# A mixer's double layer norm: two square roots and a product, or one combined scale

## The chip, the cores and the metric

The kernel runs on one core of a Trainium2 chip. Its time is device microseconds of one execution, as a median over runs. The engines named below are PE (TensorE: matmuls; PEld its weight loads), DVE (VectorE), ACT (ScalarE), POOL (GpSimd) and SP (SyncE, which here issues DMAs). Each engine works through its own queue of instructions in order and waits on semaphores for the others.

## The reference

The program is two transformer-like layers over x of 4 x 1024 x 256 in float32. What matters here is the first step of layer 0, a recurrent mixer with gates. Its input is normalized twice: once by the block and once by the mixer.

```python
def _layernorm(x, axis=-1, eps=1e-05):
    m = jnp.mean(x, axis=axis, keepdims=True)
    v = jnp.var(x, axis=axis, keepdims=True)
    return (x - m) / jnp.sqrt(v + eps)
...
    # in _L0_attn_ref, EPS = 1e-05
    mu = jnp.mean(x, axis=-1, keepdims=True)
    var = jnp.mean(jnp.square(x - mu), axis=-1, keepdims=True)
    xn = (x - mu) * jax.lax.rsqrt(var + EPS) * ln_w + ln_b
    log_i, log_f, z, o = ...                # four gates, each from xn by a 256 x 64 matrix
    # a scan over the 1024 steps: m = max(m + lf, li); c = exp(..) * c + exp(..) * z; h = o * tanh(c)
    return jnp.einsum('bsn,dn->bsd', h_seq, Wp) + bp
...
x = x + _L0_attn_ref(_layernorm(x, axis=-1), ...)      # the mixer
x = x + _L0_ffn_ref(_layernorm(x, axis=-1), ...)       # 8 experts, the best 2 of each token
x = x + _L1_attn_ref(_layernorm(x, axis=-1), ...)      # attention, 16 heads
x = x + _L1_ffn_ref(_layernorm(x, axis=-1), ...)       # 32 experts, the best 4, and a shared one
```

After the first norm the mean is 0 and the variance is var / (var + eps), so that both norms together are one scale of (x - mean): with r1 = 1 / sqrt(var + eps) and r2 = 1 / sqrt(var r1^2 + eps), it is r1 r2 = 1 / sqrt(var (1 + eps) + eps^2).

## The kernel before

x stays in SBUF, one tile of 128 partitions per batch element, with two further columns of each row for its mean and its variance or scale. Layer 0 is worked in four *units*: a pair of batch elements (0 and 1, or 2 and 3) times a half of the 1024 steps, so eight tiles of 128 tokens each. `l1_unit(u)` is the mixer of a unit, `l2_route(u)` its choice of experts. The calls stand in this order: `l1_unit(0)`, `l1_unit(1)`, `l2_route(0)`, `l2_route(1)`, the lists of the tiles of the experts' queues that are full by then (A: 25 tiles), then the same for units 2 and 3 and the lists of the other tiles (B and C), and then the experts, `l2_experts`, over 68 tiles.

A mixer unit goes: `stats` (BN statistics on DVE, L260 and L261, into the columns of x); the scale, in the lines that the change touches (L304 to L312; `rstd0` has the square root on ACT in L269 and the reciprocal on DVE in L270); `transposed`, which makes xn = (x - mean) * scale on DVE (L279), transposes it on PE (L287) and copies it out on ACT with ln_w and ln_b (L316); the addition of the output's bias to x (L323); the four gates' matmuls (L334); on DVE and ACT the clipping (L340, L341), tanh and sigmoid (L343), two scans (L356, L363) and exponentials (L359, L361, L367); and the output's matmuls (L376), added to x (L383). The route of a unit goes through `stats`, `rstd0` and `transposed` as well, then router matmuls (L396), the best two of each row (L407, L410, L412), positions in the queues by matmuls (L426, L427), and DMAs on POOL that scatter the rows of x to DRAM (L245). After the last route `pn_all` (L461), the lengths of all queues, comes from PE, and DVE makes the lists B and C from it (L470 to L568).

An expert tile is loaded from DRAM by a DMA on SP (L578), normalized on DVE (L586), transposed (L591), copied (L593), and goes through the hidden layer (L608, `ph1` and `ph2`), SiLU on ACT (L613), a product on DVE (`hid`, L614), a transposition (L620, L622) and the output (L628, L632). `ph1` and `ph2` have one PSUM bank each, so that a tile's hidden layer waits for the product of the tile before. Until tile 12 the outputs share banks with the transposed inputs; from then on they have two banks that the mixer held before (`T_LATE = 12`).

The program is recorded in this order, and a scheduler then lays the instructions out for each engine: it may put the beginning of one part between the steps of another. So expert tiles of list A stand among the instructions of units 2 and 3, on PE, DVE and ACT. The order inside the experts is kept on PE. Before attention there is a branch for tiles past the 68th (L775). Attention and layer 1's experts, after it, have an order that is written out by hand; no line of them is changed.

ACT has its functions in sets; the program has a table load where the next function is not in the set that is loaded. Square root, tanh and sigmoid, exp, and SiLU alternate in this part.

Of the kernel before, what the change touches and what calls it, by code (L numbers as in the profile page):

```python
# [14 lines left out]
F32 = mybir.dt.float32  # L15
BF16 = mybir.dt.bfloat16
I32 = mybir.dt.int32
AF = mybir.ActivationFunctionType
# [5 lines left out]
P = 128  # L24
# [4 lines left out]
EPS = 1e-5  # L29
# [27 lines left out]
def block_kernel(  # L57
# [23 lines left out]
    nc = tc.nc  # L81
    const = ctx.enter_context(tc.tile_pool(name="const", bufs=1))
# [10 lines left out]
    for pr in range(B // 2):  # L93
# [6 lines left out]
    make_identity(nc, ident)  # L100
    eps_t = const.tile([P, 1], F32, name="eps_t")
    nc.gpsimd.memset(eps_t, EPS)


    lower = const.tile([P, P], F32, name="lower0")
# [2 lines left out]
        out=lower, in_=lower, compare_op=ALU.is_gt, fill=0.0, base=0,  # L108
# [68 lines left out]
    with ExitStack() as ph:  # L177
# [3 lines left out]
        sm = ph.enter_context(tc.tile_pool(name="l2_small", bufs=2))  # L181
# [8 lines left out]
        HT0 = NT // 2  # L190
# [64 lines left out]
        def stats(u, name):  # L255

            pr, hf = units0[u]
            for b, i in tiles_of(u):
                st = sm.tile([P, 6], F32, name=f"st_{name}_{b}_{i}", tag="st", bufs=4)
                nc.vector.bn_stats(st, x[b][:, i, :D])  # L260
                nc.vector.bn_aggr(x[b][:, i, D : D + 2], st)  # L261
            half = slice(hf * HT0, (hf + 1) * HT0)
            return [x[2 * pr + par][:, half, D + 1] for par in range(2)]

        def rstd0(var, out, name):

            for par in range(2):
                r = sm.tile([P, HT0], F32, name=f"r_{name}_{par}", tag="r", bufs=4)
                nc.scalar.activation(r, var[par], AF.Sqrt, bias=eps_t)  # L269
                nc.vector.reciprocal(out[par], r)  # L270

        def transposed(u, name, evacuate):

            tiles = tiles_of(u)
            for par in range(2):
                xns = []
                for b, i in tiles[par * HT0 : (par + 1) * HT0]:
                    xn = sm.tile([P, D + 2], F32, name=f"xn_{name}_{b}_{i}", tag="xn", bufs=4)[:, :D]
                    nc.vector.tensor_scalar(  # L279
                        xn, x[b][:, i, :D], x[b][:, i, D : D + 1], x[b][:, i, D + 1 : D + 2],  # L280
                        ALU.subtract, ALU.mult,
                    )
                    xns.append(xn)
                for c in range(NC_):
                    pt = ps_t.tile([P, HS], F32, name=f"pt_{name}_{par}_{c}", tag="t")
                    for q in range(HT0):
                        nc.tensor.transpose(  # L287
                            pt[:, q * P : (q + 1) * P], xns[q][:, c * P : (c + 1) * P], ident
                        )
                    evacuate(c, par, pt)  # L290
# [7 lines left out]
        def l1_unit(u):  # L298
            pr, hf = units0[u]
            nm = f"l1_{u}"  # L300
            var = stats(u, nm)


            r1 = [sm.tile([P, HT0], F32, name=f"r1_{u}_{par}", tag=f"r1_{par}") for par in range(2)]  # L304
            rstd0(var, r1, nm)
            v2 = [sm.tile([P, HT0], F32, name=f"v2_{u}_{par}", tag=f"v2_{par}") for par in range(2)]
            for par in range(2):
                nc.vector.tensor_mul(v2[par], r1[par], r1[par])
                nc.vector.tensor_mul(v2[par], v2[par], var[par])
            rstd0(v2, v2, nm + "b")  # L310
            for par in range(2):
                nc.vector.tensor_mul(var[par], v2[par], r1[par])  # L312
            xT = xtp.tile([P, 2, NC_, HS], F32, name=f"l1_xT{u}", tag="xT")
            transposed(
                u, nm,
                lambda c, par, pt: nc.scalar.activation(  # L316
                    xT[:, par, c, :], pt, AF.Identity,
                    bias=lnwb_t[:, c, 1:2], scale=lnwb_t[:, c, 0:1],
                ),
            )  # L320
            for par in range(2):
                xs = x[2 * pr + par][:, hf * HT0 : (hf + 1) * HT0, :D]
                nc.vector.tensor_tensor(  # L323
                    xs, xs, bp_t.unsqueeze(1).to_broadcast([P, HT0, D]), ALU.add
                )

            gates = [
                big.tile([P, HS], F32, name=f"l1_{n}{u}", tag=f"g_{n}") for n in ("i", "f", "z", "o")
            ]
            for g in (1, 0, 2, 3):  # L330
                pg = ps_g.tile([P, HS], F32, name=f"pg_{u}_{g}", tag="g")
                for c in range(NC_):
                    for par in range(2):
                        nc.tensor.matmul(  # L334
                            pg[par * N0 : (par + 1) * N0, :], wgate_t[:, c, g, :], xT[:, par, c, :],
                            start=(c == 0), stop=(c == NC_ - 1),
                        )
                bias = bgate_t[:, g : g + 1]
                if g < 2:
                    nc.vector.tensor_scalar(gates[g], pg, bias, -20.0, ALU.add, ALU.max)  # L340
                    nc.vector.tensor_scalar_min(gates[g], gates[g], 20.0)  # L341
                else:
                    nc.scalar.activation(  # L343
                        gates[g], pg, AF.Tanh if g == 2 else AF.Sigmoid, bias=bias
                    )
            li, lf, z, o = gates
            m = big.tile([P, HS + 1], F32, name=f"l1_m{u}", tag="m")
            cst = li
            last = sm.tile([P, 2], F32, name=f"l1_last{u}", tag="last")
            if hf == 0:  # L350
                nc.vector.memset(m[:, 0:1], 0.0)
                m0 = c0 = 0.0
            else:
                m0, c0 = carry[pr][:, 0:1], carry[pr][:, 1:2]
                nc.vector.tensor_copy(m[:, 0:1], m0)
            nc.vector.tensor_tensor_scan(m[:, 1:], lf, li, m0, ALU.add, ALU.max)  # L356
            nc.vector.tensor_add(lf, lf, m[:, :HS])
            nc.vector.tensor_sub(lf, lf, m[:, 1:])
            nc.scalar.activation(lf, lf, AF.Exp)  # L359
            nc.vector.tensor_sub(li, li, m[:, 1:])  # L360
            nc.scalar.activation(li, li, AF.Exp)  # L361
            nc.vector.tensor_mul(z, z, li)
            nc.vector.tensor_tensor_scan(cst, lf, z, c0, ALU.mult, ALU.add)  # L363
            nc.vector.tensor_copy(last[:, 0:1], m[:, HS : HS + 1])
            nc.vector.tensor_copy(last[:, 1:2], cst[:, HS - 1 : HS])
            carry[pr] = last
            nc.scalar.activation(cst, cst, AF.Tanh)  # L367
            nc.vector.tensor_mul(o, o, cst)
            for q in range(0, HT0, 2):
                pos_ = [  # L370
                    ps_g.tile([P, 2, D], F32, name=f"po_{u}_{q}_{par}", tag="g") for par in range(2)
                ]
                for k in range(2):
                    for par in range(2):
                        rows = slice(par * N0, (par + 1) * N0)
                        nc.tensor.matmul(  # L376
                            pos_[par][:, k, :], o[rows, (q + k) * P : (q + k + 1) * P],
                            wp_t[rows, :], start=True, stop=True,
                        )
                for par in range(2):  # L380
                    i = hf * HT0 + q
                    xs = x[2 * pr + par][:, i : i + 2, :D]
                    nc.vector.tensor_add(xs, xs, pos_[par])  # L383

        def l2_route(u):
            tiles = tiles_of(u)
            nm = f"l2_{u}"
            var = stats(u, nm)
            rstd0(var, var, nm)
            xT = xtp.tile([P, 2, NC_, HS], F32, name=f"l2_xT{u}", tag="xT")  # L390
            transposed(u, nm, lambda c, par, pt: nc.scalar.copy(xT[:, par, c, :], pt))
# [309 lines left out]


        l1_unit(0)
        l1_unit(1)
        l2_route(0)
        l2_route(1)
# [17 lines left out]


        l1_unit(2)
        l1_unit(3)
        l2_route(2)
# [539 lines left out]
    with ExitStack() as ph:  # L1268
        wat = ph.enter_context(tc.tile_pool(name="w_att", bufs=1))
        sm = ph.enter_context(tc.tile_pool(name="l3_small", bufs=3))  # L1270
# [14 lines left out]
            out=mask[:, 3 * P :], in_=mask[:, 3 * P :], compare_op=ALU.is_ge, fill=-MASKED, base=0,  # L1285
# [16 lines left out]
        for p in range(NP - 1):  # L1302
            for k, src in enumerate((w_q, w_k, w_v)):
                nc.sync.dma_start(
                    out=w_pairs[:, p, k], in_=src[:, :, (p + 1) * P : (p + 2) * P]
# [624 lines left out]
```

## Time and profile before

| | us |
|---|---|
| median of 5 runs | 2044.32 |
| lowest and highest | 2043.84, 2051.47 |
| the profiled execution | 2041.24 |
| its span, first to last instruction | 2039.5 |
| PE, DVE, ACT, POOL busy in the span | 1841.4, 1253.0, 959.2, 269.4 |
| mean granted clock of PE | 0.953 |
| first and last square root of the mixer and the routes (L269) | 8.0, 175.7 |
| `pn_all` on PE | 195.0 |
| first matmul of attention | 594.28 |

A span counts from the first to the last instruction of the program. In a timeline each row has the start, the time until the end of the group, the engine, the line of the kernel, the operation, output and input with shapes, the count, and in brackets the idle time of the engine before it with what ended that. A float32 matmul can be two records. PEclk and "granted clock" are shares of PE's full clock. Rows of one engine overlap a little: the next instruction starts before the last one's result is written.

### The profile page before, as it was taken

Reading aid. Unit: us, or ns where it says so; the run is one execution under the profiler, and the core shown is the slowest. Engines: PE = TensorE matmul, PEld = TensorE weight load, DVE = VectorE, ACT = ScalarE, POOL = GpSimd, SP = SyncE. Lnnn points to the kernel's source line nnn. Section 1 sums busy time; section 2 is a strip of 40 time slices with the busy share of each in tenths; the row PEclk is TensorE's granted clock in tenths of the full one; section 3 lists DMA queues with packets and bytes.
Section 4 is the critical chain, followed back from the end, with each engine's and each line's share of the span. In section 5 each row is a group of like instructions: output and inputs, shape, how many; then the busy total and the mean of one; then the engine's idle time right before and its main releaser. Section 6 shows DMA issues by size and latency. Waiting matters only on the chain.

```text
span 2039.5 us, 45184 instructions
## 1 busy us (share of the span) xinstructions
PE 1841.4 (90%) x17612; PEld 1205.4 (59%) x17612; DVE 1253.0 (61%) x4101; ACT 959.2 (47%) x2486; POOL 269.4 (13%) x307
## 2 busy tenths in 40 slices
PE   5668899999999999999998999998999999998963
PEld 2435466665656766666665666665666665665642
DVE  6687222244227777755677675577777477777566
ACT  3354222222236665763555654456565355655210
POOL 0334400022003200000003030000302003031022
PEclk8578999999999999999999999999999999999987
DMA  9122211122135433100000000000000000002135
GB/s 350 40 65 80 90 47 47 42 80 77 54 94 162 146 116 107 64 1 2 1 2 23 2 2 2 1 2 2 2 2 2 2 2 2 2 2 70 42 127 184
DMA packets 87151, 109.23 MB, mean 54 GB/s; under 512 B 13838, under 2 KB 76650, under 8 KB 85776
## 3 DMA queue, kind: packets, MB, share of 16 engines
q1 hardware_dynamic: 66528, 73.41, 10.9%
q0 software_dynamic: 15168, 27.05, 4.4%
q10 hardware_dynamic: 5232, 5.78, 0.9%
q8 instruction: 143, 2.34, 0.5%
q14 instruction: 80, 0.66, 0.1%
HBM read 51.75 MB, written 64.77 MB: 57 GB/s over the span
## 4 chain that ended last, share of the span: by engine, by line
PE 52%; DVE 12%; ACT 3%; DMA 2%; issue 1%; SPq 0%; POOL 0%; DVEq 0%; ACTq 0%; POOLq 0%
PE ps L1452 10%; PE pa L1538 9%; PE pt L1502 7%; PE pq L903 6%; PE pz L903 5%; PE pk L903 5%; PE pv L903 5%; DVE ps L1468 3%; ACT pe L1481 3%; DMA xs_d<-x,row_l 1%; PE s_l L903 1%; DVE pT L1523 1%; DVE nm L1466 1%; PE sy L903 1%; PE pb L1409 0%
## 5 line engine op out<-in xcount | busy, mean ns | idle before, releaser
L1481 ACT ACTIVATE pe<-ps,nm 128x512 f32<-128x512 f32 (+3 forms) x768 | 439.0, 578 | 287.5 <-DVE nm L1468 282.5
L1538 PE MATMUL pa<-pT,v 128*64 128x128 f32 (+1 forms) x4096 | 325.2, 291 | 0.0
L1538 PEld LDWEIGHTS pa<-pT,v 128*64 128x64 f32 x4096 | 243.4, 138 | 102.5 <-issue 84.4
L1452 PE MATMUL ps<-k,q 64*128 64x512 f32 (+3 forms) x1536 | 296.3, 502 | 0.0
L1502 PEld LDWEIGHTS pt<-ident,pe 64*128 64x128 f32 x4608 | 206.5, 141 | 115.0 <-issue 53.9
L1502 PE MATMUL pt<-ident,pe 64*128 64x64 f32 x4608 | 240.9, 230 | 28.9 <-ACT pe L1481 28.5
L608 PE MATMUL ph<-w_t,xgT 128*128 x544 | 257.7, 615 | 7.0 <-DVE hid L614 5.8
L1523 ACT COPY pT<-pt 128x512 f32<-128x512 f32 (+2 forms) x384 | 179.3, 520 | 163.9 <-PE pt L1502 162.2
L1466 DVE TENSOR_REDUCE nm<-ps 128x1 f32<-128x512 f32 x256 | 175.8, 687 | 122.7 <-PE ps L1452 121.6
L859 POOL DMA_INDIRECT xs_d<-x,row_l x104 | 103.0, 990 | 1035.5 <-DVE second L1011 984.9
L1523 DVE COPY pT<-pt 128x256 f32<-128x256 f32 (+3 forms) x384 | 178.1, 505 | 0.0
L1452 PEld LDWEIGHTS ps<-k,q 64*128 64x128 f32 x1536 | 134.2, 190 | 66.5 <-issue 54.2
L1468 DVE CUSTOM_DVE_ANT_0 ps<-ps,mask_a,nm 128x128 f32<-128x128 f32 (+3 forms) x256 | 143.2, 559 | 40.5 <-DVE nm L1466 8.5
L608 PEld LDWEIGHTS ph<-w_t,xgT 128*128 128x128 f32 x544 | 100.7, 196 | 110.1 <-issue 102.4
L1481 ACT ACTIVATION_READ_ACCUMULATOR pe<-ps,nm 128x1 f32 x768 | 152.2, 198 | 0.0
L903 PE MATMUL pq<-l_xT,w_pairs 128*64 128x512 f32 x448 | 112.5, 624 | 30.9 <-ACT pe L1481 30.9
L1468 DVE CUSTOM_DVE_ANT_0 ps<-ps,mask_a 128x128 f32<-128x128 f32 (+3 forms) x256 | 119.7, 517 | 24.2 <-PE ps L1452 22.4
L903 PE MATMUL pz<-wo_t,y 128*64 128x256 f32 x1024 | 115.0, 379 | 0.0
L903 PE MATMUL pv<-w_pairs,l_xT 128*64 128x128 f32 x1792 | 108.9, 274 | 2.9 <-ACT pe L1481 2.9
L628 PE MATMUL py<-w_t,hidT 128*128 x464 | 109.6, 379 | 0.0
L903 PE MATMUL pk<-l_xT,w_pairs 128*64 128x512 f32 x448 | 107.2, 599 | 0.5 <-ACT pe L1481 0.5
L680 POOL DMA_INDIRECT yg<-yq_d,back x64 | 60.6, 947 | 334.0 <-issue 231.1
(412 smaller groups left out, 2228.3 us busy)
## 6 DMA issues: line engine op xcount, KB each, us to landing
yt_d<-zeros SPq DMA_DIRECT2D x32, 512.0 KB, 3.2
xg<-xe_d SPq DMA_DIRECT2D x68, 129.0 KB, 2.1
yq_d<-ys SPq DMA_DIRECT2D x68, 128.0 KB, 2.0
xs_d<-zeros SPq DMA_DIRECT2D x65, 131.5 KB, 2.2
w_t<-w_dram SPq DMA_DIRECT2D x8, 1024.0 KB, 13.2
w_pairs<-e_w_dram POOLq DMA_DIRECT2D x12, 384.0 KB, 3.7
x<-x_in_dram SPq DMA_DIRECT2D x8, 512.0 KB, 8.5
w_t<-w_dram SPq DMA_DIRECT2D x8, 512.0 KB, 13.6
```

Source lines behind the costliest of these rows:

```text
L608: nc.tensor.matmul(pt, xgT[:, c, :], w[:, c, k * H0 : (k + 1) * H0], start=(c == 0), stop=(c == NC_ - 1),)
L628: nc.tensor.matmul(py, hidT[:, c, :], w[:, c, :], start=(c == 0), stop=(c == H0 // P - 1))
L680: gather = nc.gpsimd.indirect_dma_start(out=yg, out_offset=None, in_=yq_d[: rows * P, :], in_offset=bass.IndirectOffsetOnAxis(ap=back_i[:, ...
L859: i = nc.gpsimd.indirect_dma_start(out=self.out, out_offset=bass.IndirectOffsetOnAxis(ap=idx, axis=0), in_=src, in_offset=None, bounds_che ...
L903: nc.tensor.matmul(out[r], lhsT[:, r], rhs, start=start, stop=stop)
L1452: nc.tensor.matmul(t[:, :n], qs[b, p][rows, i * P : (i + 1) * P], ks[b, p][rows, kc * 512 : kc * 512 + n], start=True, stop=True,)
L1466: nc.vector.tensor_reduce(m[:, 0:1], t, AX.X, ALU.min)
L1468: nc.vector.tensor_tensor_reduce(out=t[:, :n], in0=t[:, :n], in1=mask[:, 512 - n :], scale=1.0, scalar=-LOWEST if kc == 0 else m[:, 0:1], ...
L1481: inst = nc.scalar.activation(pe[:, :n], sps.pop((u, k, par))[:, :n], AF.Exp, bias=ms[u, i, par][:, 1:2], scale=-1.0, accum_out=ls[b, p][: ...
L1502: nc.tensor.transpose(pts[u][r][:, j, par, :], pes[u, k, par][rows, j * P : (j + 1) * P], ident[rows, rows],)
L1523: copy(to, pts[u][r][:, :n])
L1538: nc.tensor.matmul(pas[0][rows, cols], vs[b, p][:, j, rows], pTs[u][:, j, par, a * P :], start=(j == 0), stop=(j == nb - 1),)
```

## The change

The two square roots, two reciprocals and three products per batch element of a unit become one square root, with a scale of 1 + EPS and a bias of EPS^2, and one reciprocal, straight into x's column. A constant tile is added for the bias.

```diff
     eps_t = const.tile([P, 1], F32, name="eps_t")
     nc.gpsimd.memset(eps_t, EPS)
+    eps2_t = const.tile([P, 1], F32, name="eps2_t")
+    nc.gpsimd.memset(eps2_t, EPS * EPS)
...
-        def rstd0(var, out, name):
+        def rstd0(var, out, name, scale=1.0, bias=eps_t):
 
             for par in range(2):
                 r = sm.tile([P, HT0], F32, name=f"r_{name}_{par}", tag="r", bufs=4)
-                nc.scalar.activation(r, var[par], AF.Sqrt, bias=eps_t)
+                nc.scalar.activation(r, var[par], AF.Sqrt, bias=bias, scale=scale)
                 nc.vector.reciprocal(out[par], r)
...
             var = stats(u, nm)
 
 
-            r1 = [sm.tile([P, HT0], F32, name=f"r1_{u}_{par}", tag=f"r1_{par}") for par in range(2)]
-            rstd0(var, r1, nm)
-            v2 = [sm.tile([P, HT0], F32, name=f"v2_{u}_{par}", tag=f"v2_{par}") for par in range(2)]
-            for par in range(2):
-                nc.vector.tensor_mul(v2[par], r1[par], r1[par])
-                nc.vector.tensor_mul(v2[par], v2[par], var[par])
-            rstd0(v2, v2, nm + "b")
-            for par in range(2):
-                nc.vector.tensor_mul(var[par], v2[par], r1[par])
+            rstd0(var, var, nm, 1.0 + EPS, eps2_t)
```

The scheduler lays the changed program out anew, so the order of instructions differs on PE, DVE and ACT in the whole of this part, not only at the edited lines; a few issues of expert rows on SP change places too. Line numbers after the edited lines are lower by 6.

## The prediction

> **What bounds the kernel now.** I read the page first, then a table of windows over the first 260 us, then the timelines of PE, DVE and ACT in that stretch, and last the order of the changed program's instructions, engine by engine. The page says that PE carries the kernel (90% busy, 52% of the chain), but its slices show that the first 250 us are another regime.
>
> ```profile
> PE   5668899999999999999998999998999999998963
> DVE  6687222244227777755677675577777477777566
> PEclk8578999999999999999999999999999999999987
> ```
>
> The edit lies in slices 1 to 5, where PE is not full and its clock is below full speed. The windows (us; busy time, count of records; granted clock; DMA) show it closer:
>
> ```profile
> core 0: us, PE busy (x) PEld busy (x) DVE busy (x) ACT busy (x) POOL busy (x), PEclk, DMA share, GB/s
> 60.00:80.00 20.00, 13.66 (x57) 10.79 (x55) 9.71 (x60) 3.54 (x6) 0.00 (x0) 0.50 0.00 0
> ...
> 100.00:120.00 20.00, 12.08 (x42) 6.34 (x43) 16.73 (x86) 3.69 (x7) 15.06 (x15) 0.61 0.28 99
> 120.00:140.00 20.00, 12.60 (x46) 6.11 (x44) 16.07 (x58) 15.26 (x19) 3.71 (x3) 0.74 0.24 73
> 140.00:160.00 20.00, 17.84 (x85) 8.16 (x84) 19.03 (x52) 15.47 (x19) 0.00 (x0) 1.00 0.06 14
> 160.00:180.00 20.00, 19.37 (x78) 13.21 (x78) 13.79 (x88) 7.75 (x13) 3.13 (x5) 0.74 0.25 57
> ```
>
> Units 0 and 1 with their routing run up to 101 us without any expert tile. From 129 us expert tiles (L591, L608, L620, L628) stand on PE between the steps of units 2 and 3, and PE is fuller and faster. The timelines give the places that decide:
>
> ```profile
> 100.60 0.57 PE L461 MATMUL pn_half<-run,ones 128*128 128x8 f32 x2
> ...
> 194.97 0.34 PE L461 MATMUL pn_all<-run,ones 128*128 128x8 f32 x2
> ...
> 207.39 3.75 PE L608 MATMUL ph<-w_t,xgT 128*128 x4 [5.83 <-DVE hid L614]
> ...
> 221.10 3.69 PE L608 MATMUL ph<-w_t,xgT 128*128 x8
> ...
> 227.94 3.69 PE L608 MATMUL ph<-w_t,xgT 128*128 x8
> ```
>
> ```profile
> 12.30 0.22 DVE L270 RECIPROCAL r<-r_l 128x4 f32<-128x4 f32 x2
> ...
> 14.19 1.05 DVE L279 TENSOR_SCALAR xn_l<-x 128x256 f32<-128x256 f32 x3
> ...
> 107.95 0.38 DVE L279 TENSOR_SCALAR xn_l<-x 128x256 f32<-128x256 f32 x1
> ...
> 206.66 0.67 DVE L614 TENSOR_TENSOR hid<-hid,ph 128x512 f32<-128x512 f32 x1
> ```
>
> After `pn_all` (195.0) DVE makes the lists of the remaining tiles in 11.5 us without a pause, and the product `hid` of expert tile 4 stands behind them, at 206.66. PE waits for it 5.83 us. From there on nothing of the mixer is left, and PE goes through tile after tile at a fixed pace: 227.94 - 221.10 = 6.84 us.
>
> **What is removed, as engine time.** Per unit two square roots on ACT (292 ns each) and eight small DVE instructions (two reciprocals, six products, about 155 ns each, 75 ns from start to start). Over four units: 8 x 0.29 = 2.3 us of ACT, 32 x 0.075 = 2.4 us of DVE. In the changed order ACT also has three table loads fewer: 3 x 1.28 = 3.8 us. The added memset on POOL is like the one of `eps_t` (0.10 us, at 1.07), in the idle time before the first x lands at 4.9: nothing, and 0.1 us without that cover. The scale is an immediate of a square root that is there anyway. A table load shows 1283 ns, and the ACTIVATE behind it starts 1.29 us after the load does.
>
> [...]
>
> **What of it is on the path.** Four places.
> - Unit 0: the first xn starts 14.19 - 12.30 = 1.9 us after the first reciprocal. In the new order two reciprocals (0.15), one BN aggregate (0.09) and two BN statistics (0.65) stand between: 0.9 us. Gain 1.0 us. Units 1 and 3 normalize beside the gates of units 0 and 2: nothing on the path.
> - Unit 2: tile 0's xn now stands ahead of the lists of the first half. The second xn takes the place behind them where the old order has unit 2's last product (107.28), and a product and a reciprocal ahead of it (104.11, 104.18; 0.15 us) are gone: 107.1 instead of 108.53. Gain 1.4.
> - Unit 2's gates: ACT waits 4.64 us for unit 3's statistics before its square root at 121.08, and the tanh gate's table load and the gate (122.69) are queued behind. In the new order that square root stands behind both gates. PE has the tanh gate's sums about 1.8 us (eight records of 0.227 us) before its end of gates at 122.8, so at 121.0. Gain 1.6.
> - DVE: unit 2's z product (129.70) is queued behind two expert rows that wait for their DMA (2.22 us idle, until 128.69). In the new order the five waiting expert rows stand behind the output gate and before the add of the output (L383): 5 x 0.32 = 1.6 us go there. A gain of some 2 and a loss of 1.6: I take 0, with 2 either way.
> Sum: 4.0 us that the end of unit 3's routing comes earlier.
>
> **What is moved.** This is the larger part and not in the diff. The order on PE is laid out by the scheduler, and the experts fall behind: before `pn_all` the old order has hidden-layer matmuls (L608) up to three of four of tile 4 and the outputs of tiles 0 and 1; the new one has L608 of tiles 0 to 2 alone, and no output. The product `hid` behind the lists on DVE is that of tile 4 in the old order and that of tile 2 in the new one. So when the 5.83 us wait ends, PE stands exactly two tiles further back. The pace of 6.84 holds until tile 12, whose outputs have banks of PSUM of their own (the pace is then 5.82: 575.81 to 581.63), so both are tiles of that pace: 2 x 6.84 = +13.7 us. PE has no free time later to hide it: from 240 to 540 us it is busy 295.85 of 300.
>
> How much earlier does the wait end? Besides the 4.0, it lacks two tiles' work on PE ahead of it. The bounds: all of it was on the path, 13.7 more; or none. The nearest row is the first pair of units, which has the same steps and no tile among them: from its first xn to `pn_half` 100.60 - 14.19 = 86.4 us; the second pair with its tiles, 194.97 - 107.95 = 87.0. The tiles cost that path 0.6 us: they filled holes, and the clock that they kept up paid for the rest. I take about 4 us in all. Net +13.7 - 4 = +9.7 us.
>
> **The clock.** In 60:80 PE is busy 13.66 of 20 us and gets 0.50; in 140:160 it is busy 17.84 and gets 1.00. Fewer tiles in 120:180 mean more time at half clock there, as in the first pair; the 86.4 us hold that already, at its worst. A further price, if the hole after `pn_all` grows or its matmuls run at half clock: the four records at 207.39 took 3.75 us, 1.8 more than the four at 199.58 (1.98); three such stretches are +5.
>
> [...]
>
> **Rivals.**
> - *The second pair is bound by PE.* For it: PE is busy 37.2 of 40 us in 140:180. Then two tiles fewer ahead of the wait bring it 13.7 us earlier, the same 13.7 come back later, and the 4.0 of the shorter chain remain: 2044.3 - 4.0 = 2040.3, not slower. Against it: 87.0 against 86.4. It decides if the wait ends over 13.7 us earlier; to show as faster it must be 19.8.
> - *Half of the moved work was on the path*: wait ends 9 to 10 us earlier, net +4, 2048.
> - *Colder*: the chain gains only unit 0's 1.0 us, and some stretches at half clock are added: +12.7 to +18, 2057 to 2062.
> - *A later stage swallows the shift*: attention's first matmuls (594.28) wait 0.83 us for the branch behind the experts and nothing else; little speaks for it.
>
> **Numbers.** The profiled execution took 2041.24 us (span 2039.5 and 1.7 around it), 3.1 below the median of five, 2044.32. With +9.7 it would be 2050.9; on the median, 2054.0, my prediction. What a measurement can tell from no change is about 0.3%, 6.1 us. Forecast, +6 to +14: 0.56. Colder: 0.18. Half, PE-bound up to 6.1 us gain, or swallowed: 0.19. Faster by more, if the chain was worth more than 4.0 and PE bound it: 0.07. Slower 0.74, same 0.19, faster 0.07. Range: up to colder's 2062, down to 2044, so that half is in and only the cases with no loss, and little above, are out.
>
> **What would show it.** Right: in the profile after, the wait of PE for `hid` (L608 in the new lines) lies some 4 us earlier than 207.39, it is tile 2's product on DVE that ends it, and two more steps at the pace of 6.84 follow than before; the experts end near 604 instead of 594; ACT has 29 table loads instead of 32 in that part. Wrong: the wait ends 10 or more us earlier, or PE shows windows with clock 1.00 in 60:120, or the experts end at 594 and the difference lies in attention.

## The result, and the profile after

The changed kernel took 2051.77 us (median of 34 runs, 2047.64 to 2057.97), the kernel before 2044.76 us in 60 runs beside it (2037.29 to 2052.64). The ratio of the runs is 1.0034 with a 95% interval from 1.0026 to 1.0042, or +7.0 us (+5.3 to +8.6): slower by 0.3%. Here and below, the us beside a ratio are that ratio taken of the median of before; the bare difference of two medians can differ from it by up to 3 us. The forecast was 2054.0, range 2044 to 2062, likeliest sign slower.

The profiled execution took 2051.93 us with a span of 2050.3, 10.8 more than the span before. The profiled execution before lay 3.5 us below its median, so the pair of traces shows more than the runs do. The page of the changed kernel, its slices:

```profile
span 2050.3 us, 45138 instructions
...
PE   5567999999999999999999999998999999998963
...
DVE  6687222234317777654677775577777477777666
...
PEclk9567999999999999999999999999999999999986
```

PE has 5 and 7 in slices 2 and 4 where it had 6 and 8, and 9 in slice 5 where it had 8; the clock has 6 and 7 in slices 3 and 4 where it had 7 and 8; DVE's first eight digits are the same. From slice 6 on PE is as full as before. The table of windows (busy time and records of each engine, granted clock, DMA) for the same stretches:

```profile
core 0: us, PE busy (x) PEld busy (x) DVE busy (x) ACT busy (x) POOL busy (x), PEclk, DMA share, GB/s
60.00:80.00 20.00, 13.31 (x55) 10.66 (x54) 9.75 (x62) 3.48 (x6) 0.00 (x0) 0.50 0.00 0
100.00:120.00 20.00, 13.16 (x48) 6.48 (x49) 16.38 (x79) 4.32 (x6) 15.29 (x16) 0.62 0.29 103
120.00:140.00 20.00, 12.20 (x45) 6.99 (x43) 18.55 (x57) 12.93 (x16) 3.60 (x3) 0.64 0.21 63
140.00:160.00 20.00, 15.89 (x71) 9.68 (x67) 12.83 (x37) 10.92 (x15) 0.00 (x0) 0.76 0.00 1
160.00:180.00 20.00, 17.71 (x57) 9.31 (x57) 15.69 (x95) 8.26 (x11) 7.27 (x9) 0.76 0.33 83
```

60:80 and 100:120 are nearly as before. From 120 on PE does less, and 140:160, which had a clock of 1.00, has 0.76. Added up from the trace's clock records, 115 to 211 us holds 41.2 us at half clock, against 31.1 before. PE's timeline:

```profile
100.01 0.54 PE L455 MATMUL pn_half<-run,ones 128*128 128x8 f32 x2
...
190.85 0.36 PE L455 MATMUL pn_all<-run,ones 128*128 128x8 f32 x2
...
203.34 3.78 PE L602 MATMUL ph<-w_t,xgT 128*128 x4 [6.97 <-DVE hid L608]
...
217.47 3.69 PE L602 MATMUL ph<-w_t,xgT 128*128 x8
...
224.30 3.69 PE L602 MATMUL ph<-w_t,xgT 128*128 x8
...
604.29 3.65 PE L897 MATMUL pq<-l_xT,w_pair 128*64 128x512 f32 x16 [0.82 <-ACTq L769]
```

`pn_all` comes 4.1 us earlier than 194.97 and the wait for `hid` ends 4.05 earlier than 207.39; the pace is still 6.83; attention starts at 604.29 instead of 594.28, 10.0 later. In DVE's timeline the first xn (L281) and the product behind the lists (L608), which is now tile 2's:

```profile
12.47 0.23 DVE L272 RECIPROCAL x<-r_l 128x4 f32<-128x4 f32 x2
...
13.32 1.04 DVE L281 TENSOR_SCALAR xn_l<-x 128x256 f32<-128x256 f32 x3
...
106.91 0.41 DVE L281 TENSOR_SCALAR xn_l<-x 128x256 f32<-128x256 f32 x1
...
202.61 0.68 DVE L608 TENSOR_TENSOR hid<-hid,ph 128x512 f32<-128x512 f32 x1
```

ACT's timeline at the gates of unit 2: the square root of unit 3 (L271) now stands behind both gates, but ahead of the exponentials.

```profile
119.97 0.69 ACT L337 ACTIVATE l_z<-pg,bgate_t 128x512 f32<-128x512 f32 x1 [3.93 <-PE pg L328]
...
123.97 0.30 ACT L271 ACTIVATE r_l<-x,eps_t 128x4 f32<-128x4 f32 x1
124.29 1.28 ACT L353 ACT_TABLE_LOAD   x1
125.58 0.63 ACT L353 ACTIVATE l_f<-l_f 128x512 f32<-128x512 f32 x1
```

The tanh gate is 2.7 us earlier than its 122.69 before, the exponential only 1.1 earlier than its 126.69.

### The profile page after: what moved, and what is told of

It is laid out like the page before. It is cut to its first block, busy times and chain, and to the rows that moved or that the text cites. A ratio compares the mean times of both kernels' runs of the same rounds, so it can differ in the third digit from the quotient of the medians.

```text
span 2050.3 us, 45138 instructions
## 1 busy us (share of the span) xinstructions
PE 1847.3 (90%) x17612; PEld 1208.2 (59%) x17612; DVE 1250.7 (61%) x4069; ACT 954.7 (47%) x2475; POOL 269.3 (13%) x308
## 3 DMA queue, kind: packets, MB, share of 16 engines
q1 hardware_dynamic: 66528, 73.41, 10.8%
## 4 chain that ended last, share of the span: by engine, by line
PE 51%; DVE 12%; ACT 3%; DMA 2%; issue 2%; SPq 0%; POOL 0%; DVEq 0%; ACTq 0%; POOLq 0%
PE ps L1446 10%; PE pa L1532 9%; PE pt L1496 7%; PE pq L897 6%; PE pz L897 5%; PE pk L897 5%; PE pv L897 5%; DVE ps L1462 3%; ACT pe L1475 3%; DMA xs_d<-x,row_l 1%; PE s_l L897 1%; DVE pT L1517 1%; DVE nm L1460 1%; PE sy L897 1%; PE pb L1403 0%
```

## Experiments: which edit moves the tiles, and what the move costs

The theory is the prediction's: the time is lost because two expert tiles move behind the list tail on DVE (the 11.5 us of lists after `pn_all`). Rival 1 puts the price into the edited arithmetic, or into the colder clock around each edited unit. Rival 2 says that PE bounds the second pair, so that the order of the tiles makes no difference. The first four kernels ran beside 35 runs of before, with a median of 2043.42.

**Unit 3 alone.** With a condition on the unit, the single scale can be given to some units only:

```diff
-            rstd0(var, var, nm, 1.0 + EPS, eps2_t)
+            if u == 3:
+                rstd0(var, var, nm, 1.0 + EPS, eps2_t)
+            else:
+                ... (the two square roots and products as before)
```

> The single scale in unit 3 alone; units 0 to 2 keep the two square roots. The scheduler lays this out like the whole change: three tiles' hidden layers (12 matmuls of L608's kind) before pn_all, and tile 2's product behind the list tail. Theory (order): two tiles of 6.84 us go behind the list tail, +13.7, and only the gain at unit 2's gates (1.6, the square root of unit 3 behind them) and little else comes back: +9 to +13 us against before, that is above the +7.0 of the whole change, and experts that end 10 or more us later. Rival 1 (the price sits in the edited arithmetic or in the colder clock that each edited unit makes): a quarter of the whole change, about +2. Rival 2 (PE bounds the second pair, and the order changes nothing): -1.6 to 0.

Measured: 2052.96 us, ratio 1.0032 (1.0015 to 1.0049), +6.5 us (+9.5 between the medians). PE's timeline of it:

```profile
192.86 0.36 PE L466 MATMUL pn_all<-run,ones 128*128 128x8 f32 x2
...
205.33 3.78 PE L613 MATMUL ph<-w_t,xgT 128*128 x4 [6.95 <-DVE hid L619]
...
606.23 3.65 PE L908 MATMUL pq<-l_xT,w_pair 128*64 128x512 f32 x16 [0.82 <-ACTq L780]
```

A quarter of the edit has the whole loss, with the same wait of 6.95 us. In the trace attention starts 11.95 us later than before, as the theory has it; by the ratio the loss equals that of the whole change and is not above it, so the theory's +9 to +13 is met by the trace and the medians only. A quarter of the whole loss (rival 1, about +2) lies outside the interval, and so does rival 2.

**Units 0 to 2** (`u < 3` in the same place).

> The single scale in units 0, 1 and 2; unit 3 keeps the two square roots. The scheduler then leaves the tiles about where they were: 16 hidden-layer matmuls before pn_all (19 before the change, 12 in the whole change), outputs of tiles 0 and 1 before it, and tile 4's product behind the list tail as in the old order. Theory (order): nothing is pushed back, and unit 0's 1.0 and unit 2's 1.4 us are gained: -2 to -4 us against before. Rival 1 (the price sits in the arithmetic or in the clock): three quarters of the whole change, about +5. Rival 2 (PE bound, order without effect): -2 to 0, so this run does not tell it from the theory.

Measured: 2043.80 us, ratio 0.9997 (0.9979 to 1.0015), -0.6 us. Rival 1's +5 is outside the interval. The gain of 2 to 4 is inside it but not shown by the runs. The trace has it, and shows where it went:

```profile
192.79 0.35 PE L466 MATMUL pn_all<-run,ones 128*128 128x8 f32 x2
...
205.53 2.91 PE L613 MATMUL ph<-w_t,xgT 128*128 x4 [3.49 <-DVE hid L619]
...
591.07 3.65 PE L908 MATMUL pq<-l_xT,w_pair 128*64 128x512 f32 x16 [0.83 <-ACTq L780]
```

Attention starts 3.2 us earlier than before, but from there to the end of the span it takes 1456.2 us instead of 1445.3, with 106.8 us of them at half clock against 87.8. This part of the program is not edited. One window of that stretch, first of before and then of this kernel (columns as in the table above):

```profile
1100.00:1400.00 300.00, 282.06 (x3375) 189.24 (x3371) 204.96 (x642) 166.22 (x468) 25.48 (x26) 0.99 0.02 4
```

```profile
1100.00:1400.00 300.00, 282.32 (x3295) 187.77 (x3293) 203.40 (x640) 163.10 (x461) 25.42 (x26) 0.97 0.01 4
```

PE is busy just as long, and gets through 80 fewer records, 2.4%; that fits the clock (the column 0.99, then 0.97). The same kernel was profiled and run a second time, to see whether that is chance.

> The same kernel as the one with the single scale in units 0 to 2, a second profile and a second set of runs. Theory (order): experts end 2 to 4 us earlier than the 594.28 of before as in its first profile (591.07); what the runs show beyond that is where the half-clock stretches of layer 1 fall, which differs from run to run, so the two sets of runs put together should lie 2 to 4 us below before. If layer 1 takes 10 us more in this profile too (from 591.07 to the end it took 1456.1 us, against 1445.3 in before), the loss there is not chance, and the gain is given back later.

Measured: 2170.94 us, beside 35 runs of before at 2174.08: this set ran on another chip, where the kernel before takes some 130 us longer (see the last section). Ratio 0.9984 (0.9968 to 1.0000), -3.5 us. The two sets are -0.6 and -3.5, -2 on average: at the lower end of what was expected, and neither interval is clear of zero. The profile was of no use for the question of layer 1, since on that chip the granted clock of every run of this set is lower, 0.921 to 0.934 against 0.946 to 0.956 in the runs of the first kernels.

**The old arithmetic, with two tiles held back.** One dependency is added:

```diff
+                    if (t, k, c) == (2, 0, 0):          # first hidden matmul of tile 2
+                        wait_for(i, pn_all.name, "hold")
```

> The old arithmetic; the one edit is that the hidden layer of tile 2 and all tiles after it stand on PE behind pn_all, so that tile 2's product is the one behind the list tail, as in the changed kernel. Theory (order): two tiles at 6.84, +13.7, less what pn_all comes earlier because tiles no longer stand in its way (0 to 4): +9 to +14. Rival 1 (arithmetic): 0, nothing of it is changed. Rival 2 (PE bounds the second pair): pn_all comes as much earlier as the tiles take, 0.

Measured: 2050.35 us, ratio 1.0036 (1.0021 to 1.0051), +7.4 us. PE's timeline:

```profile
192.56 0.54 PE L462 MATMUL pn_all<-run,ones 128*128 128x8 f32 x2
193.03 6.02 PE L609 MATMUL ph<-w_t,xgT 128*128 x8
...
205.25 1.98 PE L609 MATMUL ph<-w_t,xgT 128*128 x4 [0.95 <-DVE hid L617]
...
602.75 3.65 PE L906 MATMUL pq<-l_xT,w_pair 128*64 128x512 f32 x16 [0.83 <-ACTq L778]
```

Not one instruction of the normalization differs from before, and the loss is that of the change. Rival 1's 0 and rival 2's 0 are outside the interval. It is a little below the range of the theory: attention starts 8.5 us later. The SiLU of tile 12, with which the tiles' pace changes, is at 267.0 us, 9.7 later than before; in the changed kernel it is 10.0 later. `pn_all` comes 2.4 us earlier than before, with no arithmetic saved: that is what the tiles had cost on the path, net of the clock (from 115 to 211 us this kernel has 45.2 us at half clock, before had 31.1). The wait of PE for tile 2's product is only 0.95 us here, since it does tile 2's whole hidden layer (6.02 us) beside the lists.

**The changed arithmetic, with two tiles put ahead again.**

```diff
+                    if (t, k, c) == (4, 0, 1):          # half of tile 4's hidden layer
+                        wait_for(pn_all, i.name, "ahead")
```

> The whole change, with pn_all on PE put behind the first half of tile 4's hidden layer: 18 hidden-layer matmuls and the outputs of tiles 0 and 1 before it, tile 4's product behind the list tail, as in the old order. Theory (order): the two tiles come back. If they fit into the holes of the second pair as in the old order, -13.7 against the changed kernel, which is -4 to -7 against before; if half of them push pn_all back, 0 against before. Rival 1 (arithmetic or clock): stays at +7. Rival 2 (PE bounds the second pair): pn_all is later by all of the tiles' time, and the time stays at +7 too; then the wait for hid ends some 13 us later than the 203.3 of the changed kernel, where the theory has 204 to 210.

Measured: 2044.28 us, ratio 1.0003 (0.9990 to 1.0016), +0.6 us against before, so 6.4 less than the whole change.

```profile
203.35 0.28 PE L456 MATMUL pn_all<-run,ones 128*128 128x8 f32 x2
...
214.47 1.99 PE L625 MATMUL pxy<-w_t,hidT 128*128 x8 [1.75 <-DVE xgT L588]
...
596.20 3.65 PE L900 MATMUL pq<-l_xT,w_pair 128*64 128x512 f32 x16 [0.83 <-ACTq L772]
```

With this order the loss is gone, against rival 1's +7. But it is not the old order. Up to the last `pos` matmul (191.13 us, 190.42 in the changed kernel) PE's order is nearly that of the changed kernel; the work put ahead stands in one block from 191.4 us to `pn_all`, which is 12.5 us later, as rival 2 had it. So whether the tiles would fit into the holes of the second pair was not tried. Its time (+7) still did not follow. DVE's order has changed as well: tile 4's product, which was expected behind the lists, stands among them, and the copy of tile 6's input (L588) and tile 5's product stand behind them.

```profile
206.16 0.68 DVE L611 TENSOR_TENSOR hid<-hid,ph 128x512 f32<-128x512 f32 x1
...
214.01 0.41 DVE L588 COPY xgT<-pxy 128x256 f32<-128x256 f32 x1
...
214.63 0.68 DVE L611 TENSOR_TENSOR hid<-hid,ph 128x512 f32<-128x512 f32 x1
```

The longest wait of PE behind `pn_all` is now 1.75 us instead of 6.97. So part of what the order decides is what PE has to do while DVE makes the lists.

**The lists moved away.** What a tile behind the list tail costs should then depend on that tail. In the next kernels the lists B and C and the rows' way back are queued on DVE in four parts, behind the products of tiles 2, 4, 6 and 8; they are first needed for the load of tile 25. The scatters of padding rows, DMAs that POOL issues, move with the first part:

```diff
-        ... (lists B, C and the way back, right behind pn_all)
+        def tail1(): ...     # the padding rows and the counts;  tail2: list B;  tail3: list C;  tail4: the way back
...
         def behind(t):
+            if t in tails:
+                with tc.issue_after(hid_ins[t]):
+                    tails[t]()
```

They ran in two sets on the slower chips, the first beside 35 runs of before (2174.08), the second beside 30 (2174.51). The first set:

> The whole change, with the lists B and C and the rows' way back taken out of the place behind pn_all and queued on DVE in four parts behind the products of tiles 2, 4, 6 and 8. No product stands behind 11.5 us of lists any more. Theory (order: what a tile that is pushed back costs is set by the list tail, since from there on PE has no hole): the wait of 6.97 us is gone and the four matmuls behind it run at full clock (1.8 us), each part of the lists (about 3 us) hides beside 6.84 us of PE: -8 to -10 us against the changed kernel, -1 to -3 against before, and the step of the tiles stays at 6.84. Rival 1 (the price sits in the arithmetic or in the clock of the second pair): the lists cost PE nothing by themselves and the time stays at +7. Rival 2 (the tail only moves: each part of the lists makes PE wait beside its tile): four waits of some 1 to 2 us in place of one, -1 to -3 against the changed kernel.

> The kernel before, with the same move of the lists behind the products of tiles 2, 4, 6 and 8. Theory (order): the wait of 5.83 us is gone and 1.8 us at half clock with it: -7 to -9 us against before. If the price of the change is only the tiles that go behind the list tail, then without that tail the two arithmetics differ by less than the +7 they differ by now: 4 to 8 us with three tiles against 4.75 ahead of pn_all, and most of it if PE has no holes in the second pair. Rival 2 (the tail only moves): -1 to -3.

> The single scale in units 0 to 2, which leaves the tiles in the old order, and the lists queued behind the products of tiles 2, 4, 6 and 8. Theory (order): both gains add, 5.83 + 1.8 from the wait and 2 to 4 from the shorter chain: -9 to -12 us against before, faster than both kernels, with the first matmul of attention at 582 to 585. Rival 1 (arithmetic or clock): no faster than before. Rival 2 (the tail only moves): -3 to -6.

Measured against before: the change with late lists 2174.58 us, 0.9996 (0.9980 to 1.0011), -0.9 us; before with late lists 2169.73, 0.9983 (0.9968 to 0.9998), -3.7 us; units 0 to 2 with late lists 2168.60, 0.9977 (0.9961 to 0.9993), -5.0 us. The order of the three is as expected. The last two gained about half of what was expected. PE is held up for 14.7 us from 228.5 us on in the last of them; such a stop of 12.2 to 16.7 us, in one piece or two, lies between 224 and 252 us in every trace of these chips, also where the lists stand right behind `pn_all`. For units 0 to 2 this set has both placements of the lists, and moving them gained little: 2.3 us by the medians (2170.94 and 2168.60), 1.5 at the start of attention (619.17 and 617.68). PE's wait behind the lists was only 2.17 us there:

```profile
220.67 3.25 PE L613 MATMUL ph<-w_t,xgT 128*128 x4 [2.17 <-DVE desc_C L537]
```

The changed kernel itself was missing on these chips, so the second set has it:

> The whole change again, to stand beside the kernels with late lists on one chip. Theory (order): +7 against before, as in the runs that gave the result; the first matmul of attention 8 to 12 us later than in before. On a chip where POOL's indirect DMAs hold the other engines up (14.7 us on PE at the lists in the last set of runs) the two tiles may cost another amount, since the place behind pn_all is where that happens: 0 to +13.

> The whole change with the lists behind the products of tiles 2, 4, 6 and 8, beside the whole change on one chip. Theory (order): the wait of 6.97 us and 1.8 us at half clock are gone, -8 to -10 us against the changed kernel. Rival 1 (arithmetic or clock): no difference between the two. Rival 2 (the tail only moves): -1 to -3.

> The kernel before with late lists, beside the changed one with late lists. Theory (order): the wait of 5.83 us goes and no other comes in its place: -4 to -9 us against before (the last set gave -3.7 with an interval from -7.0 to -0.4, on a chip that held PE up by 14.7 us at this place). The wait of PE for the product of tile 4 is under 1 us. Rival 2 (the tail only moves): -1 to -3, with waits of 1 to 2 us at tiles 2, 4, 6 and 8.

> The single scale in units 0 to 2 and late lists. Theory (order): the gain of late lists and 2 to 4 us of the shorter chain: -7 to -12 us against before, the fastest of the four; the last set gave -5.0 (-8.5 to -1.5). Rival 1 (arithmetic or clock): not faster than the kernel before with late lists.

| | us | ratio to before (95%) | us against before | first matmul of attention |
|---|---|---|---|---|
| the change | 2183.30 | 1.0038 (1.0020 to 1.0055) | +8.3 | 639.14 |
| the change, late lists | 2174.05 | 0.9994 (0.9982 to 1.0005) | -1.3 | 628.56 |
| before, late lists | 2169.82 | 0.9983 (0.9971 to 0.9995) | -3.7 | 623.23 |
| units 0 to 2, late lists | 2168.24 | 0.9971 (0.9956 to 0.9985) | -6.3 | 622.38 |

PE's timeline of the change, of the change with late lists and of before with late lists:

```profile
225.14 3.47 PE L602 MATMUL ph<-w_t,xgT 128*128 x4 [5.90 <-DVE desc_C L526]
...
249.98 0.69 PE L585 MATMUL pxy<-ident,xg 128*128 128x128 f32 x2 [12.38 <-ACT ys L626]
...
639.14 3.65 PE L897 MATMUL pq<-l_xT,w_pair 128*64 128x512 f32 x16 [0.83 <-ACTq L769]
```

```profile
230.60 0.69 PE L585 MATMUL pxy<-ident,xg 128*128 128x128 f32 x2 [6.05 <-ACT ys L626]
...
246.63 0.69 PE L585 MATMUL pxy<-ident,xg 128*128 128x128 f32 x2 [7.97 <-ACT ys L626]
...
628.56 3.65 PE L917 MATMUL pq<-l_xT,w_pair 128*64 128x512 f32 x16 [0.83 <-ACTq L789]
```

```profile
220.28 3.69 PE L608 MATMUL ph<-w_t,xgT 128*128 x8 [0.25 <-issue]
...
248.12 0.69 PE L591 MATMUL pxy<-ident,xg 128*128 128x128 f32 x2 [15.16 <-issue]
```

The change costs +8.3 here (7 runs; there is no profile of the kernel before on these chips to set its 639.14 against). Late lists take 9.3 us off it by the medians (9.6 by the ratios, 10.6 in the traces), the 8 to 10 of the theory; rival 1 had no difference, rival 2 at most 3. Not all of it is shown to be the list tail's: in the traces `pn_all` itself comes 3.3 us earlier with late lists (209.16 and 212.50), after a shorter stop of PE ahead of it (6.91 and 10.73 us), and moving the lists made the scheduler put some 3 us more of tile work ahead of it. Late lists take only 3.7 off the kernel before, a little under the 4 to 9, though no wait for a product of over 1 us is left behind its `pn_all`. Between the two arithmetics, both with late lists, 2.4 us remain by the ratios (2.8 in the first set), 4.2 by the medians and 5.3 at the first matmul of attention, instead of 8.3. So some of the price goes with the list tail, by the runs half or more; with intervals of 2.5 to 4 us each way, how much is not settled.

The single scale in units 0 to 2 with late lists is faster than both kernels, 0.9971 of before, a little short of the -7 to -12 expected. That it beats before with late lists (-2.6 us between them, and 0.85 us at the start of attention) is not shown: the difference is smaller than the intervals.

## Why the prediction was right, step by step

- **Sign, size, mechanism.** Two tiles go behind the list tail and cost more than the arithmetic saves. The trace has attention 10.0 us later; the sum said +9.7, and that it came so near is partly luck (third point). The held-back kernel (+7.4 without any new arithmetic, tile 12 9.7 us later), unit 3 alone (+6.5) and the tiles put ahead (+0.6 with all of it) show that the order is the cause.
- **Two tiles at 6.84.** Tile 12's SiLU is at 267.3 instead of 257.3 us, 10.0 later, although the wait ends 4.05 earlier: 14.05 where 13.7 was forecast.
- **The 4.0 us of the chain.** `pn_all` and the end of the wait are 4.1 and 4.05 earlier: the sum is right, its terms are not. The steps that were priced came out at 0.9 (first xn, forecast 1.0), 1.6 (unit 2's xn, 1.4) and 1.1 rather than 1.6 at unit 2's gates, where the moved square root and a table load now stand ahead of the exponential; unit 2's second scan is 2.6 us earlier in all. In the fourth place, put at 0, the z product is 2.4 us earlier (127.29), and five expert rows take 1.7 us behind the output gate's product. Arithmetic with the tiles about in their old places (units 0 to 2, three of 19 hidden-layer matmuls fewer ahead of `pn_all`) brings `pn_all` forward by 2.2, and tiles held back with the old arithmetic by 2.4. So about half of the 4.1 is what the tiles no longer cost on the path, and that term had been put at next to nothing, from the 0.6 us between the first pair and the second. Two errors of about 2 us cancelled, which is luck.
- **The clock.** Colder it was: 41.2 us at half clock between 115 and 211, against 31.1. It did not reach the rival's price, since the chain still ended earlier. But it is part of the loss: 10.1 us more at half clock are at most 5 us of PE's work (an estimate: half of them, as four `ph` records took 3.75 us before at a clock of 0.52, and 1.98 at 1.00), of the 10.0 by which attention is later. The sum has this inside its two tiles at 6.84. The runs change the order and do not separate how much of the delay is idle PE and how much is clock. The further price, a longer hole behind `pn_all`, did not come: the wait is 6.97 us against 5.83, and the four matmuls behind it took 3.78 us, as 3.75 before.
- **Table loads.** Three fewer, as forecast: 27 instead of 30 up to 210 us (the forecast's count was 29 instead of 32). The next ACTIVATE starts 1.29 us after the load again (124.29 to 125.58).
- **The number.** 2054.0 was the median plus 9.7, and 2051.77 was measured. The +7.0 of the runs stands against +10.7 between the two profiled executions, because that of before was 3.5 us under its median. The runs of before alone spread over 17 us (2036.84 to 2054.12). Their granted clock tells most of it: in the 35 runs beside the first four kernels, the four at 0.954 have spans of 2035.2 to 2041.5 us, the seven at 0.951 2042.1 to 2045.2, the one at 0.946 2052.5. The profiled execution of before (2039.5 at 0.953) lies among the five at 0.953, 2038.5 to 2042.4: an execution with a little more clock than most.
- **The rivals.** PE as the bound of the second pair is refuted (held tiles cost +7.4). That two tiles forced ahead pushed `pn_all` back by 12.5 us does not tell for or against it, since they were laid in one block right ahead of it. A later stage swallowed nothing: from the start of attention to the end of the span it is 1446.0 us, against 1445.3.

## What to carry to other kernels

An edit that only removes instructions can lose time where a scheduler lays the program out again: compare the order on each engine first, and count how many units of the bounding engine's work end up behind the next long block of another engine. A block that nothing needs for a while (here 11.5 us of lists, needed some 20 tiles later) is worth trying in small parts beside the bounding engine's work: that took 9.6 us off the changed kernel and 3.7 off the kernel before, while the arithmetic alone (units 0 to 2) gained some 2 us, not clear of zero. A gain of two or three microseconds at the place of the edit can be seen in the trace, and lost in the total, when the spread of the runs is 17.

## What the hardware showed that was not expected

- **Most of the spread goes with the clock, and the clock's stretches lie elsewhere in each execution.** The granted clocks of the 35 runs above show the first (a span of 2052.5 us at 0.946, 2035.2 to 2041.5 at 0.954). The first stretch at full clock on record begins at 23.3, 23.1, 21.5, 22.1, 23.7 and 20.5 us in the six traces of the first chip, and the later edges follow in steps of 3.41 us: the stretches at half clock last 1, 2, 3, 4, 5, 6, 10, 16 or 17 such steps (but for one near the end). How many fall in layer 1 differs between executions: it takes 1445.3 us with 87.8 at half clock in before and 1456.2 with 106.8 in units 0 to 2, though 1445.1 with 80.8 in unit 3 alone.
- **On two other chips the same program takes 130 us longer**, 2174.5 against 2044.8 us; in the traces of the changed kernel 35 us of it lie ahead of attention and 101 behind. In these traces PE stops for 5 to 17 us at a time, and ACT and DVE do little, while POOL issues indirect DMAs (in the changed kernel PE is busy 1.61, DVE 0.69, ACT 0.59 and POOL 7.56 of the 10 us from 236 to 246 us), and what the profile names as ending it is each other, "issue" or "remote". The waits of the changed kernel between 186 and 252 us there:

```profile
engine line waited for: us in total, times, longest us
ACT hidT L616 <- remote: 18.5, 2, 10.7
DVE sc L397 <- remote: 14.5, 1, 14.5
```

  The same comes back in layer 1. Two windows of units 0 to 2 with late lists:

```profile
1120.00:1130.00 10.00, 4.45 (x23) 2.07 (x22) 0.69 (x1) 0.00 (x0) 7.57 (x9) 0.73 0.15 48
1130.00:1140.00 10.00, 8.37 (x40) 4.45 (x41) 3.29 (x6) 2.80 (x6) 2.84 (x3) 0.50 0.08 27
```

  DVE is busy 0.69 us and ACT not at all while POOL is busy 7.57, and half clock follows. What holds the engines up was not tried; that POOL's indirect DMAs do, as the expectation of the changed kernel's second set has it, was the author's reading. POOL's issuing alone is not shown to do it: in the changed kernel on the first chip POOL is busy 7.70 of 10 us from 206 to 216 us, and PE 9.29. The comparisons above are each made on one chip.
